# Local deformable attention: one dense read per tile, one write per head, values stored by quarters, loads on ScalarE's queue

## Chip, core and metric

The kernel runs on one core of a Trainium2 chip. The metric is the device time of one execution in microseconds. Before the change three runs took 7693.72, 7705.02 and 7705.33 us; their median, 7705.02 us, is the time to which the change is compared.

The engines by their names in the profile: PE is TensorE (matmuls and transposes; PEld are its weight loads), DVE is VectorE, ACT is ScalarE, POOL is GpSimd, SP is SyncE, which only issues DMAs. ACT issues DMAs too, in order with its own arithmetic (ACTq in the profile).

## What is computed

The program is a network of four blocks, each a "conv" stage and a feed-forward stage with layer norms and residuals, on an input of 4 x 64 x 64 x 128 numbers in float32. Only the first stage, deformable attention, is touched. Cut to what matters:

```python
# q, k, v: layer norm, 1x1 conv, depthwise 3x3 conv; 4 heads g of 32 channels, dilations 1, 3, 5, 7
# per head: 9 taps, each with an offset (y, x) and one mask, made from q by small convs
k_s = deform_sample(k, offset, mask, dilation, pad)   # bilinear: 4 neighbours, 0 outside the image
v_s = deform_sample(v, offset, mask, dilation, pad)
attn = softmax(sum_c(q * k_s) * 32 ** -0.5)           # over the 9 taps
out = sum_taps(attn * v_s);  y = proj(out) + x
```

A sampled value is a weighted sum of pixels. When every offset is at most 1 in size, the pixels that a tap can touch are a 3 x 3 patch around its undisturbed place, with weights that are products of a "hat" in y and a "hat" in x. This is the local part; a branch at run time takes a general path where an offset is larger. With the given inputs the local part runs.

## The kernel before, in words

`stage_deformable` (L366) has two parts.

**Projection** (`deformable_project`, L394 to L606). For each of 4 images: norm (L478, its inputs loaded at L483), q, k, v by matmul and depthwise matmuls (L514), stores to device memory: queries `qd`, keys `kd` (L529), values `vd` (L571, [column, row, channel] with a zero border), offsets and masks `od` (L594). It then reduces the largest offset and loads it into registers (L606), and the branch follows.

**Local part** (`deformable_near`, L609 to L970). A tile T is 128 pixels (two image rows), a chunk c is four tiles; there are 128 tiles and 32 chunks. Its stages:

- `hats` and `hat_products` (L688, L705; POOL): the hats of a chunk from its offsets, times the masks `mk`, and their 3 x 3 products `H`, nine weights per tap.
- `products` (L713; POOL) copies the queries of one tile into a zero-padded weight tile `qm`, of which there are two. `product` (L738; PE, 32 matmuls by 4 heads x 2 halves x 4 blocks, 64 records per tile at L750) multiplies it by bands of keys; `copy_products` (L756; ACT) moves the four results from PSUM to `band`. PSUM has one set of these accumulators, so the next tile's `product` waits for this copy.
- `attention` (L762; DVE): a band covers more columns and rows than a pixel needs; predicated copies shift it by pixel, one copy by row (L768, by bit 3 of the partition's masks) and three by columns (L771, by 4, 2 and 1). Then come the products with `H` (L775), the sum (L782) and the softmax's maximum.
- `spread` (L795): ACT takes the exponential (L798), DVE normalises and writes attn x H into `A`, laid out per pixel as a window of columns with 4 rows (L805 to L818). Partitions of odd image rows are written one row further on by the DMA (`3 * r` in L829).
- `write` (L820; SP): `A` to a scratch memory `dd`, 16 DMAs per chunk (4 heads x 4 groups of 32 partitions), two scratch memories per head in turn.
- `read_dense` (L833): `dd` is read back with each partition's start moved by one pixel, which makes a dense row of weights over a common window of pixels: 4 DMAs per tile, heads 0 and 2 on SP's queue and heads 1 and 3 on ACT's.
- `value_block` (L842; SP): a block of 4 image rows of values, 4 DMAs of 256 KB, one for each quarter q of the columns.
- `transpose` (L862; PE, copies `dt` by ACT), `weigh` (L874; PE, 96 small matmuls), then per chunk the copy of the output (L900), the load of the input `xg` for the residual (L904, SP), its sum with the bias (L905, POOL), `projection` (L908) and, one step later, `store` (L918, SP).

**The order.** The loop of L934 runs steps T = 0 to 141. In a step it emits the stages of different tiles: `products(T+1)`, `hats`, `attention`, `spread`, `write` of chunks at steps 0, 4, 7 and 9 after their first tile, `read_dense` 12 steps and `transpose`/`weigh` 14 steps (`LAG`) after. `behind()` ties the PE blocks to their order and all else behind the last block. The framework's planner turns this into one instruction list per engine from its own cost estimates; each engine then works through its list in order and waits where data or a buffer isn't there. So a DMA that must wait also holds what stands behind it on its engine. Inputs of the local part (`of`, `q`, `kpad`) are loaded at L686, L736 and L729, all by SP.

Of the kernel before, what the change touches and what calls it, by code (L numbers as in the profile page):

```python
# [365 lines left out]
def stage_deformable(k, x, y, w_qkv, b_qkv, w_dw, b_dw, pconv, w_offT, b_off, grid, masks, w_proj, b_proj):  # L366
# [13 lines left out]
    with ExitStack() as octx:  # L380
# [6 lines left out]
        far = deformable_project(k, fp, x, qd, kd, vd, od, w_qkv, b_qkv, w_dw, b_dw, pconv, w_offT, b_off)  # L387
        with tc.If(far > 0) as branch:
            deformable_general(k, x, y, w_qkv, b_qkv, w_dw, b_dw, pconv, w_offT, b_off, grid, w_proj, b_proj)
        with branch.Else():  # L390
            deformable_near(k, dr, x, y, qd, kd, vd, od, masks, w_proj, b_proj)


def deformable_project(k, fp, x, qd, kd, vd, od, w_qkv, b_qkv, w_dw, b_dw, pconv, w_offT, b_off):  # L394
# [9 lines left out]
    with ExitStack() as ctx:  # L404
# [129 lines left out]
        for b in range(4):  # L534
# [57 lines left out]
            for i in range(4):  # L592
                r, h = divmod(i, 2)
                nc.sync.dma_start(od[b][64 * h + 32 * r : 64 * h + 32 * r + 32], off[32 * i : 32 * i + 32])  # L594

# [13 lines left out]
def deformable_near(k, dr, x, y, qd, kd, vd, od, masks, w_proj, b_proj):  # L609
# [23 lines left out]
    PP = [12 * (15 + w) for w in W]  # L633
    with ExitStack() as ctx:
# [14 lines left out]
        for t in qms:  # L649
            nc.gpsimd.memset(t, 0.0)  # L650

# [5 lines left out]

        dd = [[dr.tile([128, 4 * PP[g] + 12], F32, tag=f"dd{i}{g}", name=f"dd{i}{g}") for g in range(4)] for i in range(2)]

        dense = [wp.tile([128, 4, 384], F32, tag=f"D{i}", name=f"D{i}") for i in range(4)]  # L660
        for t in dense:
            nc.gpsimd.memset(t, 0.0)
        for i in range(2):
            for g in range(4):
                zero = dense[g].rearrange("p t n -> p (t n)")
                eng = (nc.sync, nc.scalar)[g % 2]
                eng.dma_start(dd[i][g][:, 0 : 4 * PP[g]], zero[:, 0 : 4 * PP[g]])
                eng.dma_start(dd[i][g][:, 4 * PP[g] : 4 * PP[g] + 12], zero[:, 0:12])

        Hs, bands, outs, vblocks, logits, ofs, hat_of, queries = {}, {}, {}, {}, {}, {}, {}, {}  # L670
        accs, lefts, project, stores = {}, {}, [], []
        last = [None]
# [10 lines left out]
        def offsets(c):  # L683
            b, c8 = divmod(c, 8)
            ofs[c] = sm.tile([128, 4, 81], F32, tag="of", name="of")
            nc.sync.dma_start(ofs[c], od[b][:, 4 * c8 : 4 * c8 + 4, :])  # L686

        def hats(c):  # L688
# [10 lines left out]
            mk = sm.tile([128, 3, 4, 3], F32, tag="mk", name="mk")  # L699
            nc.gpsimd.tensor_copy(mk, window(of, 72, [[3, 3], [81, 4], [1, 3]]))  # L700
            hy = hat[:, 0:4].rearrange("p s a t n i -> p s (a t n) i")
            nc.gpsimd.tensor_tensor(hy, hy, window(mk, 0, [[0, 4], [1, 36], [0, 3]]), op=ALU.mult)
            Hs[c] = sm.tile([128, 4, 36, 9], F32, tag="H", name="H", bufs=3)

        def hat_products(c, groups):  # L705
            H, hat = Hs[c], hat_of[c]
            for g in groups:
                nc.gpsimd.tensor_tensor(
                    H[:, g].rearrange("p n (a c) -> p n a c", a=3), window(hat, 108 * g, [[3, 36], [1, 3], [0, 3]]),
                    window(hat, 108 * (4 + g), [[3, 36], [0, 3], [1, 3]]), op=ALU.mult,  # L710
                )
# [14 lines left out]
        def rows_of_keys(n):  # L726

            b, h = divmod(n, 4)
            nc.sync.dma_start(  # L729
                kpad[:, 8 + 16 * h : 24 + 16 * h, 8:72], kd[b].rearrange("p (y x) -> p y x", x=64)[:, 16 * h : 16 * h + 16, :]  # L730
            )

        def rows_of_queries(n):
            b, h = divmod(n, 8)
            queries[n] = sm.tile([128, 8, 64], F32, tag="q", name="q")
            nc.sync.dma_start(queries[n], qd[b].rearrange("p (y x) -> p y x", x=64)[:, 8 * h : 8 * h + 8, :])  # L736
# [25 lines left out]
        def attention(c):  # L762
            H, band = Hs[c], bands.pop(c)
            prod = sm.tile([128, 4, 36, 9], F32, tag="prod", name="prod", bufs=1)
            for g in range(4):
                rows = lambda off, dims: window(band[g], off, [[4 * CW[g], 12]] + dims)
                n = 3 * CW[g]
                nc.vector.copy_predicated(rows(0, [[1, n]]), bit[:, 0, :, 3:4].to_broadcast([128, 12, n]), rows(CW[g], [[1, n]]))  # L768
                for i, s in enumerate((4, 2, 1)):
                    n = W[g] + s - 1  # L770
                    nc.vector.copy_predicated(  # L771
                        rows(0, [[CW[g], 3], [1, n]]), bit[:, :, :, i : i + 1].to_broadcast([128, 12, 3, n]), rows(s, [[CW[g], 3], [1, n]])
                    )
                for tx in range(3):
                    nc.vector.tensor_tensor(  # L775
                        window(prod, 324 * g + 9 * tx, [[27, 12], [3, 3], [1, 3]]),
                        window(band[g], DIL[g] * tx, [[4 * CW[g], 12], [CW[g], 3], [1, 3]]),
                        window(H, 324 * g + 9 * tx, [[27, 12], [3, 3], [1, 3]]), op=ALU.mult,
# [16 lines left out]
        def spread(c):  # L795
# [7 lines left out]
            for g in range(1, 4):  # L803
                for ty in range(3):
                    nc.vector.tensor_tensor(  # L805
                        window(A[g], ty, [[12 * DIL[g], 12], [3, 3], [12, 3]]), window(H, 324 * g + 108 * ty, [[9, 12], [3, 3], [1, 3]]),
                        window(lg, 36 * g + 12 * ty, [[1, 12], [0, 3], [0, 3]]), op=ALU.mult,
                    )

            t0 = sm.tile([128, 36, 9], F32, tag="t0", name="t0", bufs=1)  # L810
            nc.vector.tensor_tensor(t0, H[:, 0], window(lg, 0, [[1, 36], [0, 9]]), op=ALU.mult)
            for ty in range(3):
                a0 = lambda m0, n: window(A[0], 12 * m0 + ty, [[60, 4], [12, n], [3, 3]])
                tap = lambda tx, s0, n: window(t0, 108 * ty + 9 * tx + s0, [[27, 4], [1, n], [3, 3]])
# [5 lines left out]
        def write(c):  # L820
            A = As[c % 2]
            for g in (1, 2, 3, 0):
                d, P = dd[c % 2][g], PP[g]
                for j in range(4):
                    r = j % 2
                    nc.sync.dma_start(
                        bass.AP(
                            d.tensor, d.offset + 32 * j * (4 * P + 12) + 3 * r, [[4 * P + 12, 32], [P, 4], [1, 12 * W[g]]]
                        ),  # L829
                        A[g][32 * j : 32 * j + 32, :, 0 : W[g]].rearrange("p t c s a -> p t (c s a)"),  # L830
                    )

        def read_dense(T):  # L833
            c, t = divmod(T, 4)
            for g, d in enumerate(DIL):
                m, P = dd[c % 2][g], PP[g]
                (nc.sync, nc.scalar)[g % 2].dma_start(
                    dense[t][:, g, 12 * (7 - d) : 12 * (7 - d) + P],
                    bass.AP(m.tensor, m.offset + t * P, [[16 * (4 * P + 12), 8], [4 * P, 16], [1, P]]),
                )  # L840

        def value_block(n):  # L842
# [4 lines left out]
            d = vd[b]  # L847
            for q in range(4):
                nc.sync.dma_start(
                    t[:, q].rearrange("p s c -> p (s c)"),  # L850
                    bass.AP(d.tensor, d.offset + 16 * q * 10752 + 4 * kb * 128, [[10752, 32], [128, 4], [1, 512]]),
                )
            vblocks[b, kb] = t

        def values(T):
# [3 lines left out]
            if T % 4 == 0:  # L859
                outs[0] = ps.tile([128, 4, 128], F32, tag="out", name="out")  # L860

        def transpose(T):  # L862
            D = dense[T % 4]
            lefts[T] = []
            for ty in range(3):
# [3 lines left out]
                dt = sm.tile([128, 4, 128], F32, tag="dt", name="dt", bufs=4)  # L869
# [4 lines left out]
        def weigh(T):  # L874
# [8 lines left out]
            for q in range(4):  # L883
                for n in range(3):
                    for g in range(4):
                        if n < len(taps[g]):
                            ty, kb, si = taps[g][n]
                            ins = nc.tensor.matmul(
                                quarter(outs[0][32 * g : 32 * g + 32, T % 4, :], q), vblocks[b, kb][:, q, si, 32 * g : 32 * g + 32],
# [5 lines left out]
        def values_done(T):  # L895
            b, i = divmod(T, 32)
            if T % 4 == 3:
# [5 lines left out]
                xg = sm.tile([128, 4, 128], F32, tag="xg", name="xg")  # L903
# [1703 lines left out]
```

## Time and profile before

| What | Value |
|---|---|
| Median of 3 runs | 7705.02 us |
| The profiled execution: its own time, its span | 7690.3 us, 7688.3 us |
| Mean granted clock of PE over the span | 0.892 |
| Projection | 0 to 666 us of the span |
| First `product`, first `transpose`, last `transpose` | 685.2, 778.1 and 1825.0 us |
| The other stages of the network | from about 1830 us on |
| PE, DVE, ACT, POOL busy over the span | 85%, 63%, 35%, 23% |

How to read it: the page cuts the span into 40 slices of 192 us; the local part fills slices 4 to 10. "Busy" of an engine is the time of its instructions, without waits. Beside a line of idle time stands what ended it. Times inside the span come from one profiled execution, so a sum over them is to be set against 7690.3 us, which is 14.7 us under the median of the runs.

### The profile page before, as it was taken

How to read it: one execution, taken by the hardware profiler on the slowest of the kernel's cores; microseconds unless marked ns; L12 is line 12 of the kernel's file. 1: busy time of each engine (PE TensorE's matmuls, PEld its weight loads, DVE VectorE, ACT ScalarE, POOL GpSimd, SP SyncE). 2: the span in 40 equal slices, each digit the busy share in tenths (PEclk: the TensorE clock that was granted, in tenths of full speed). 3: DMA queues.
4: the chain of work that ended last, by engine and by line, in shares of the span. 5: the costliest groups of instructions: out<-in, count | busy, mean ns of one | idle time of the engine just before them, and what ended most of it. 6: DMA issues, size and time to landing. Idle time of an engine off the chain costs nothing. (4 is left out here: it accounts for less than half of the span.)

```text
span 7688.3 us, 157708 instructions
## 1 busy us (share of the span) xinstructions
PE 6522.7 (85%) x63791; PEld 3542.4 (46%) x63791; DVE 4821.5 (63%) x11178; ACT 2690.3 (35%) x6141; POOL 1741.4 (23%) x1634
## 2 busy tenths in 40 slices
PE   7995777775688868989989999798898997997989
PEld 3343666663455644345555555445225234242244
DVE  2113766764277554858856656674785875867877
ACT  3331333333234313611146555565104013031056
POOL 0003444320001100035532221154012112120135
PEclk9997887887799889999999988798897997988989
DMA  4436677775400022030100000001111111111101
GB/s 121 98 87 179 187 209 205 213 199 172 143 4 1 2 60 48 10 117 22 27 12 10 9 10 6 9 1 30 39 25 49 26 33 40 25 35 38 25 23 31
DMA packets 678781, 495.59 MB, mean 64 GB/s; under 512 B 302326, under 2 KB 594104, under 8 KB 674200
## 3 DMA queue, kind: packets, MB, share of 16 engines
q1 hardware_dynamic: 480910, 354.59, 17.0%
q10 hardware_dynamic: 197130, 130.77, 6.2%
q8 instruction: 509, 8.34, 0.5%
q14 instruction: 232, 1.90, 0.1%
HBM read 335.28 MB, written 149.75 MB: 63 GB/s over the span
## 5 line engine op out<-in xcount | busy, mean ns | idle before, releaser
L2476 DVE TENSOR_TENSOR t<-S,q 128x1536 f32<-128x1536 f32 (+3 forms) x608 | 1156.9, 1948 | 123.2 <-PE S L2464 117.9
L2464 PE MATMUL S<-R,L 32*128 32x512 f32 x4096 | 734.6, 651 | 90.3 <-DMA R<-wd 78.9
L2492 PE MATMUL acc<-t,sum 128*32 128x512 f32 x4096 | 639.5, 608 | 0.0
L750 PE MATMUL S<-kpad,qm 32*64 32x240 f32 (+3 forms) x8192 | 403.4, 421 | 216.0 <-ACT band L760 97.5
L2178 PE MATMUL pe<-ew,yT 128*128 128x512 f32 x1024 | 479.4, 603 | 27.4 <-DVE xs L2184 24.5
L1777 PE MATMUL acc<-w,attT 128*64 128x264 f32 x4096 | 486.3, 391 | 10.4 <-DVE w L1773 10.4
L2464 PEld LDWEIGHTS S<-R,L 32*128 32x128 f32 x4096 | 200.6, 186 | 611.4 <-issue 280.4
L2498 ACT COPY agg<-acc 128x512 f32<-128x512 f32 x32 | 18.8, 586 | 1194.0 <-DMA L<-pd 626.7
L750 PEld LDWEIGHTS S<-kpad,qm 32*64 32x64 f32 x8192 | 299.9, 156 | 271.5 <-issue 136.9
L1770 POOL TENSOR_TENSOR w<-xtl,ei 128x528 f32<-128x528 f32 x256 | 332.1, 1319 | 309.6 <-ACT ei L1769 204.5
L2184 DVE SCALAR_TENSOR_TENSOR xs<-pe,gate,xs 128x128 f32<-128x128 f32 x1024 | 332.5, 345 | 96.5 <-PE pe L2178 79.8
L1773 DVE TENSOR_TENSOR w<-xtl,pe 128x1056 f32<-128x1056 f32 x256 | 320.3, 1251 | 100.3 <-ACT ei L1769 89.4
L1777 PEld LDWEIGHTS acc<-w,attT 128*64 128x64 f32 x4096 | 284.0, 137 | 197.5 <-DVE w L1774 38.0
L2187 ACT ACTIVATE sc<-pe,gate 128x128 f32<-128x128 f32 x1024 | 291.3, 374 | 202.2 <-PE pe L2178 194.1
L514 PE MATMUL dw<-pad,diag 32*32 32x512 f32 x6912 | 310.4, 614 | 12.9 <-issue 7.0
L2507 POOL TENSOR_TENSOR o<-o,bf 128x512 f32<-128x512 f32 x32 | 40.7, 1271 | 1229.4 <-ACT o L2506 1229.4
L760 ACT COPY band<-S 128x144 f32<-128x144 f32 (+3 forms) x512 | 136.0, 351 | 480.4 <-DMA D<-dd 152.3
L2492 PEld LDWEIGHTS acc<-t,sum 128*32 128x32 f32 x4096 | 92.7, 108 | 458.4 <-issue 436.1
L2178 PEld LDWEIGHTS pe<-ew,yT 128*128 128x128 f32 x1024 | 185.6, 193 | 234.3 <-issue 151.4
L768 DVE COPY_PREDICATED band<-bit,band 128x432 f32<-128x432 int32 (+3 forms) x128 | 107.5, 895 | 270.0 <-ACT band L760 264.2
L868 PE MATMUL pt<-ident,D 128*128 128x128 f32 x1536 | 243.0, 315 | 29.2 <-DMA D<-dd 15.2
L771 DVE COPY_PREDICATED band<-bit,band 128x288 f32<-128x288 int32 (+11 forms) x384 | 243.0, 742 | 0.0
(520 smaller groups left out, 13065.8 us busy)
## 6 DMA issues: line engine op xcount, KB each, us to landing
vb<-vd SPq DMA_DIRECT2D x272, 256.0 KB
D<-dd ACTq DMA_DIRECT2D x128, 192.0 KB
D<-dd SPq DMA_DIRECT2D x128, 168.0 KB
D<-dd ACTq DMA_DIRECT2D x128, 144.0 KB
w<-in_e_weight_dram ACTq DMA_DIRECT2D x16, 1024.0 KB
w<-in_e_weight_dram SPq DMA_DIRECT2D x16, 1024.0 KB
wd<-s SPq DMA_DIRECT2D x32, 512.0 KB
D<-dd SPq DMA_DIRECT2D x128, 120.0 KB
```

What stands on the lines that cost most here:

```text
L514: nc.tensor.matmul(acc[g][32 * c : 32 * c + 32], diag[r, j, tap, :], pads[j][r, y0 : y0 + 8, tx : tx + 64], start=(tap == 0), stop=(tap == 8),
L750: ins = nc.tensor.matmul(acc[g][64 * h : 64 * h + 64].rearrange("p (a s) c -> p a s c", a=3), qm[rows, h, m, :], keys, start=(m == 0), sto ...
L771: nc.vector.copy_predicated(rows(0, [[CW[g], 3], [1, n]]), bit[:, :, :, i : i + 1].to_broadcast([128, 12, 3, n]), rows(s, [[CW[g], 3], [1, ...
L1770: nc.gpsimd.tensor_tensor(w2[:, 2:4], xt[:, 2:4, 0:2], window(ei, 0, [[0, 2], [0, 2], [1, 132]]), op=ALU.mult)
L1773: nc.vector.tensor_tensor(w1, xt[:, :, 1:3], window(pe, 0, [[0, 4], [0, 2], [1, 132]]), op=ALU.mult)
L1777: nc.tensor.matmul(acc[b // 2][64 * (b % 2) : 64 * (b % 2) + 64], attT[:, b // 2, hp, 64 * (b % 2) : 64 * (b % 2) + 64], src[:, b].rearran ...
L2178: nc.tensor.matmul(pe[h].rearrange("p e c -> p (e c)"), yT[:, 128 * t : 128 * t + 128], ew[:, 4 * h : 4 * h + 4, :].rearrange("p e c -> p ...
L2184: nc.vector.scalar_tensor_tensor(xt, pe[0][:, e, :], gate[:, t, e : e + 1], xt, op0=ALU.mult, op1=ALU.add)
L2187: nc.scalar.activation(sc[:, e, j, :], pe[1][:, e, :], AF.Copy, scale=gate[:, t, 4 + e : 5 + e])
L2464: nc.tensor.matmul(S[:, j, :], Ls[n % 2][r, ag, :], Rs[n % 2][r, ag].rearrange("p x y -> p (x y)"), start=True, stop=True)
L2476: nc.vector.tensor_tensor(t[:, j0:j1].rearrange("p u (x y) -> p u x y", x=8), S[:, j0:j1].rearrange("p u (x y) -> p u x y", x=8), qf[:, q0 ...
L2492: nc.tensor.matmul(acc[0][32 * h : 32 * h + 32, :], sum4, t[:, j, :], start=(u < 4), stop=(u >= 60))
```

## The change

The scratch memory gets one layout for all heads: per pixel-row of 128 partitions, 4 tiles x 4 heads x 384 numbers. Four DMAs write it per chunk (one per head, all 128 partitions), one DMA per tile reads it, and there are three such memories in turn. Since a write no longer moves odd rows by one, `H` gets four rows of weights: the first three or the last three are filled, by the masks times (1 - row) and times row; the row shift (L768) goes, the column shifts work on all 48 rows of a band. Values are copied a second time in the projection, device memory to device memory, by quarters (`vq`), and a block of values is then one DMA. Loads of offsets, keys, queries and of `xg` are issued by ACT; `xg` is loaded at the start of a chunk's first `weigh` step, not after its last; offsets are loaded a step earlier; stores are issued two steps after the projection or later. `H` has 2 buffers (before 3), `dt` 3 (before 4).

```diff
+        vq = [dr.tile([32, 84, 4, 128], F32, tag=f"vq{b}", name=f"vq{b}") for b in range(4)]
...
                 nc.sync.dma_start(od[b][64 * h + 32 * r : 64 * h + 32 * r + 32], off[32 * i : 32 * i + 32])
+            for q in range(4):
+                nc.sync.dma_start(vq[b][:, :, q, :], vd[b][16 * q : 16 * q + 32])
...
-    PP = [12 * (15 + w) for w in W]
+    ROW = 4 * 4 * 384 + 12
...
-        dd = [[dr.tile([128, 4 * PP[g] + 12], F32, tag=f"dd{i}{g}", name=f"dd{i}{g}") for g in range(4)] for i in range(2)]
+        dd = [dr.tile([128, ROW], F32, tag=f"dd{i}", name=f"dd{i}") for i in range(3)]
...
-        for t in dense:
-            nc.gpsimd.memset(t, 0.0)
-        for i in range(2):
-            for g in range(4):
...
+        nc.gpsimd.memset(dense[0], 0.0)
+        zero = dense[0].rearrange("p g n -> p (g n)")
+        for d in dd:
+            for t in range(4):
+                nc.scalar.dma_start(d[:, 1536 * t : 1536 * t + 1536], zero)
+            nc.scalar.dma_start(d[:, 6144:ROW], zero[:, 0:12])
...
-            nc.gpsimd.tensor_copy(mk, window(of, 72, [[3, 3], [81, 4], [1, 3]]))
+            nc.gpsimd.tensor_copy(mk[:, 0].rearrange("p (a t n) -> p a t n", a=3, t=4), window(of, 72, [[3, 3], [81, 4], [1, 3]]))
+            nc.gpsimd.tensor_scalar(mk[:, 1], mk[:, 0], row, None, op0=ALU.mult)
+            nc.gpsimd.tensor_tensor(mk[:, 0], mk[:, 0], mk[:, 1], op=ALU.subtract)
             hy = hat[:, 0:4].rearrange("p s a t n i -> p s (a t n) i")
-            nc.gpsimd.tensor_tensor(hy, hy, window(mk, 0, [[0, 4], [1, 36], [0, 3]]), op=ALU.mult)
-            Hs[c] = sm.tile([128, 4, 36, 9], F32, tag="H", name="H", bufs=3)
+            h4 = hy_of[c] = sm.tile([128, 4, 36, 4], F32, tag="hy", name="hy", bufs=1)
+            nc.gpsimd.tensor_tensor(h4[:, :, :, 0:3], hy, at(0), op=ALU.mult)
+            nc.gpsimd.tensor_tensor(hy, hy, at(1), op=ALU.mult)
+            nc.gpsimd.tensor_tensor(h4[:, :, :, 1:3], h4[:, :, :, 1:3], hy[:, :, :, 0:2], op=ALU.add)
+            nc.gpsimd.tensor_copy(h4[:, :, :, 3], hy[:, :, :, 2])
+            Hs[c] = sm.tile([128, 4, 36, 12], F32, tag="H", name="H")
...
-                nc.vector.copy_predicated(rows(0, [[1, n]]), bit[:, 0, :, 3:4].to_broadcast([128, 12, n]), rows(CW[g], [[1, n]]))
                 for i, s in enumerate((4, 2, 1)):
                     n = W[g] + s - 1
-                    nc.vector.copy_predicated(
-                        rows(0, [[CW[g], 3], [1, n]]), bit[:, :, :, i : i + 1].to_broadcast([128, 12, 3, n]), rows(s, [[CW[g], 3], [1, n]])
-                    )
+                    nc.vector.copy_predicated(flat[:, :, 0:n], bit[:, 0, :, i : i + 1].to_broadcast([128, 48, n]), flat[:, :, s : s + n])
...
         def write(c):
-            for g in (1, 2, 3, 0):
-                for j in range(4):
...
+            for g, d in enumerate(DIL):
+                m = dd[c % 3]
+                nc.sync.dma_start(
+                    bass.AP(m.tensor, m.offset + 384 * g + 12 * (7 - d), [[ROW, 128], [1536, 4], [1, 12 * W[g]]]),
+                    As[c % 2][g][:, :, 0 : W[g]].rearrange("p t c s a -> p t (c s a)"),
+                )
...
         def read_dense(T):
-            for g, d in enumerate(DIL):
-                (nc.sync, nc.scalar)[g % 2].dma_start(
...
+            m = dd[c % 3]
+            nc.sync.dma_start(
+                dense[t].rearrange("p g n -> p (g n)"), bass.AP(m.tensor, m.offset + 1536 * t, [[16 * ROW, 8], [ROW - 12, 16], [1, 1536]])
+            )
...
         def value_block(n):
-            for q in range(4):
-                nc.sync.dma_start(
...
+            d = vq[b]
+            nc.sync.dma_start(
+                t.rearrange("p s q c -> p (s q c)"), bass.AP(d.tensor, d.offset + 4 * kb * 512, [[84 * 512, 32], [512, 4], [1, 2048]])
+            )
...
         def values(T):
...
             if T % 4 == 0:
                 outs[0] = ps.tile([128, 4, 128], F32, tag="out", name="out")
+                inputs[0] = sm.tile([128, 4, 128], F32, tag="xg", name="xg")
+                nc.scalar.dma_start(inputs[0], tokens(x, b, i, 4))
...
-                step(T, -2, offsets, 4)
+                step(T, -3, offsets, 4)
...
-            late = list(stores)
+            late = [o for o in stores if o[0] <= T - 2]
```

`rows_of_keys`, `rows_of_queries` and `offsets` change from `nc.sync` to `nc.scalar` and nothing else. In `hat_products`, `attention` and `spread` the nine weights per tap become twelve (`[3, 3]` becomes `[3, 4]` or `[4, 3]` in the access patterns), with the same number of instructions beside the removed L768.

## The prediction

> **What bounds the kernel now.** I read the slices first, to see what sort of stretch the local part is. In these rows PE's busy share, its granted clock, and the DMA engines' share stand in tenths; the local part is slices 4 to 10.
>
> ```profile
> PE   7995777775688868989989999798898997997989
> PEclk9997887887799889999999988798897997988989
> DMA  4436677775400022030100000001111111111101
> ```
>
> PE is busy for 7 tenths, at a clock of about 8, while the DMA engines are busy for 7 tenths too: nothing is full. The second view gives the busy time of PE, PEld, DVE, ACT and POOL in four stretches, then clock, DMA share and GB/s:
>
> ```profile
> 224.00:273.00 49.00, 47.52 (x353) 14.78 (x354) 11.55 (x75) 32.61 (x64) 0.00 (x0) 0.93 0.22 61
> 690.00:780.00 90.00, 48.76 (x863) 36.87 (x871) 65.76 (x139) 17.62 (x61) 65.87 (x82) 0.70 0.69 203
> 780.00:1750.00 970.00, 733.11 (x19481) 612.47 (x19464) 645.76 (x1629) 327.05 (x878) 379.88 (x541) 0.83 0.72 204
> 1750.00:1830.00 80.00, 53.38 (x1594) 46.96 (x1592) 19.53 (x57) 28.25 (x55) 8.10 (x7) 0.85 0.56 168
> ```
>
> The steady stretch, 780 to 1750 us, holds tiles 14 to 127 of the product: 114 steps or 28.5 chunks, so 970 / 28.5 = 34.0 us a chunk. Per chunk PE is busy 25.7, DVE 22.7, POOL 13.3, ACT 11.5 us, the DMA engines 0.72 x 34.0 = 24.5 us. So the period is made by waits. The list of waits in that stretch names them (who waited, for whom: total, times, longest):
>
> ```profile
> POOL xg L905 <- DMA xg<-in_x_dram: 351.3, 20, 23.4
> ACT band L760 <- DMA D<-dd: 145.6, 28, 8.3
> PE S L750 <- ACT band L760: 89.0, 41, 5.7
> ACT lg L798 <- DMA D<-dd: 82.6, 11, 9.4
> PE S L750 <- POOL qm L721: 60.6, 16, 8.4
> ACT lg L798 <- DMA kpad<-kd: 49.0, 6, 10.6
> ```
>
> L798 is an exponential; it reads neither keys nor dense rows. It stands behind a DMA issue on ACT that had to wait. The timeline of one chunk shows the whole knot:
>
> ```profile
> 1203.52 2.57 PE L750 MATMUL S<-kpad,qm 32*64 32x144 f32 x64
> ...
> 1218.27 0.46 SPq L904 DMA_DIRECT2D xg<-in_x_dram  x1
> ...
> 1220.04 1.44 ACTq L837 DMA_DIRECT2D D<-dd  x2
> 1221.52 0.32 ACT L798 ACTIVATE lg<-lg 128x144 f32<-128x144 f32 x1 [9.65 <-DMA xg<-in_x_dram]
> 1221.75 1.04 ACT L760 COPY band<-S 128x144 f32<-128x144 f32 x4
> 1222.16 4.82 PE L750 MATMUL S<-kpad,qm 32*64 32x144 f32 x64 [5.15 <-ACT band L760]
> 1223.68 1.34 POOL L905 TENSOR_TENSOR xg<-xg,bpj 128x512 f32<-128x512 f32 x1 [16.64 <-DMA xg<-in_x_dram]
> ```
>
> SP reaches the load of `xg` late, behind writes and value loads. ACT's two reads wait (by the trace's inference until that load has landed), ACT stands for 9.65 us, the accumulators aren't copied, PE waits 5.15 us, and the product after the gap takes 4.82 instead of 2.57 us. POOL meanwhile stands 16.64 us.
>
> **The change, part by part**, per chunk in the steady stretch.
>
> *DMA issues.* By the medians of the lines' own rows (write L826 431 ns, read L837 598, values L849 602, about 450 for the small loads), SP spends 16 x 0.43 + 8 x 0.60 + 8.1 x 0.60 + 3.5 x 0.45 + 0.38 (store) = 18.5 us on issuing; after, 4 x 0.43 + 4 x 0.60 + 2.0 x 0.60 + 0.38 = 5.7. ACT's 8 reads (8 x 0.58 = 4.7 us, and the waits above: 145.6 + 82.6 + 49.0 = 277 us, 9.7 a chunk) become 3.5 small loads, 1.6 us. What those wait for is old: keys for a product that the copy ahead of them on ACT waits for anyway, queries and offsets for a buffer of two chunks ago, `xg` for a store issued two steps earlier. If they do wait, the exponential, the copies to `band` and `dt` stand behind them, and PE behind these.
>
> *The load of `xg`* moves from the end of the chunk's four weighing steps to their start, on the other queue. 351 us of POOL's waiting goes, and with it most of PE's 60.6 us for `qm`. What is late next on POOL is its own work.
>
> [...] The row: the steady stretch moves 204 GB/s at a share of 0.72 through both queues together. [...] I credit the order of the load, not its queue; no term below counts bandwidth for it.
>
> *PE.* At full clock a step takes 5.0 us (transposes 1201.96 to the next ones at 1206.99, without a gap), a chunk 4 x 5.0 + 2.1 (projection, L911) = 22 us. No instruction is added.
>
> *DVE.* L768 goes: 36.4 + 31.0 + 26.0 + 21.1 = 114.5 us over 32 chunks, 3.6 a chunk. The twelve shifts grow by a third: their sizes sum to 5328 elements, so 1776 more; from 612 elements (980 ns) to 180 (527 ns) one costs 1.05 ns: +1.9. Products L775 (12 x 36 more), reduction L782 (432 more), L805 (9 x 36), L811 (108), L815 to L818 (108) have 1404 more elements, at about 1.04 ns +1.5. Sum -0.2: nothing.
>
> *POOL.* Two operations of 36 (mask copy L700: 0.33 each), a second product by the mask (L702: 1.0), one addition of 288 (L697: 0.76), a copy of 144 (between L700's 0.33 and L698's 0.63: 0.4), four products of 432 in place of 324 (1.0 against 0.815: +0.76): +3.6 us, 13.3 to 17. Within a period of 25 that hides. Where it doesn't: small copies L816 take 0.17 us alone and 0.77 beside POOL's products (median 239, longest 1290 ns), so at worst all 3.6 us fall on DVE: 22.7 to 26.3.
>
> *DMA bytes.* A dense tile grows from 192 + 168 + 144 + 120 = 624 KB to 768 KB, a chunk from 34.0 us x 204 GB/s = 6.94 to 7.53 MB. At the present 204 / 0.72 = 283 GB/s per full share this is 26.6 us; if the 5.3 MB of dense rows and values, in rows of 6 and 8 KB, run as fast as 680 to 690 us do (377 GB/s at 1.07, that is 352) and the rest as in the projection (107 at 0.46, that is 233), 15.1 + 9.6 = 24.7.
>
> *Period after.* PE 22, DVE 22.5 to 26.3, DMA 24.7 to 26.6: three within a fifth of each other never overlap wholly, and nothing above 26.6 is left as a wait of its own, so I take 27, bounds 25 and 32. Steady: 28.5 x (27 - 34) = **-200 us** (-257 to -57).
>
> *The last 14 steps* (80 us, `transpose` and `weigh` alone): one read and an earlier `xg`: -5, bounds -15 and 0.
>
> *The copies to `vq`* (16 of 1344 KB in pieces of 512 B). No row copies memory to memory. The nearest: the eight loads L554 (8 x 500 KB, pieces of 252 B) hold SP 21 us, 190 KB a us, so 5376 KB an image take 28 us; below, at 352 GB/s, 16; above, if each byte costs for reading and for writing, 56. For images 0 to 2 SP has room: after the stores L594 end at 224.5 us it has only two loads (249.7) before 273.5, and the DMA share there is 0.22. So +3 us, bounds 0 and 75 (at 56 the norm's loads come 25 us late for each). For image 3 they stand on SP ahead of the register load and the local part's first lines.
>
> *The start.* Zeros grow from 5.1 to 9.5 MB, 4.4 MB at 377 GB/s = 12 us, all on ACT, whose first copy already waits 34.8 us for them; the last `vq` copies share the engines. Against it, 16 + 16 issues per chunk shrink in a stretch of 90 us where SP spends 11.2 us on one chunk's writes and 10 on reads. I take +10, bounds -15 and +35. `dt` and `H` with a buffer less: a `dt` is free once the weighing ahead has run, `H` of two chunks ago once its spread has; POOL already waits 35 us for that in all: 0, up to +30.
>
> Sum: -200 - 5 + 3 + 10 = -192, so 7690.3 becomes 7498. The runs' median lies 14.7 us above that execution, their lowest 3.4; with about 12 of it I forecast **7510 us**.
>
> **Rivals.**
> 1. *Some of the knot stays* (0.20): another load takes the waiting place, ACT's `xg` behind its store or a read behind its four writes, which now all must land before one DMA. For it: SP stays in order, and 123 us of its waits in the stretch are writes behind dense reads. The period ends at 30 to 32: -114 to -57, so about 7595 to 7650.
> 2. *Deeper* (0.08): DVE's bound of 22.5 holds and DMA runs at its best, 24.7 a chunk: -265 and a start 15 us shorter, 7400 to 7430.
> 3. *Slower* (0.12): the `vq` copies lie open. Place: SP and the shared engines at the end of each image. Price: 4 x 56 = 224 us, against the -192: about +32, 7735. It decides from some 48 us of open time an image. Against it: the 49 us of room at 224 to 273.
> 4. *No change* (0.06): an unseen wait of PE keeps the period; "issue" ends 60 us of its idle time before L888, which the change doesn't name. 7690 to 7720.
>
> **The numbers.** The forecast (period 25 to 29) has 0.54. Faster by over 0.2% (15 us, about what a measurement of this kernel can tell): 0.54 + 0.20 + 0.08 = 0.82; within: 0.06; slower: 0.12. The range 7420 to 7650 takes the forecast, rival 1 and half of rival 2.
>
> **What the profile after should show.** `xg L905 <- DMA xg` gone from POOL's waits; no DMA ahead of L760 and L798; SP's issues for a chunk under 8 us; PE's clock in the steady stretch about 0.9, products near 2.6 us; DMA share 0.85 or more; DVE's busy time there within 5% of 646 us. Last `transpose` at about 1635 us. I am wrong if the first product starts after 720 us, if DVE's busy time grows by a tenth, or if the period is above 30 with ACT or SP still held by a DMA.

## The result and the profile after

The changed kernel takes 8020.93 us (median of 4 runs, 8003.6 to 8058.26) beside 7699.37 us (4 runs) of the kernel before: ratio 1.0425, 95% interval 1.0384 to 1.0467. The forecast was 7510. The profiled execution took 8032.4 us (span 8030.6), 342 us more than the one before.

Where the 342 us lie can be read from one pair of rows. The view of tile `xg` gives the first and the last start of POOL's sum `xg<-xg,o`, which closes each of the 32 chunks (columns: least, median and longest duration in ns, then first and last start). Before, then after:

```profile
L914 POOL TENSOR_TENSOR xg<-xg,o x32: 1262/1272/1289, 820.4 to 1829.6; 128x512 f32<-128x512 f32 x32
```

```profile
L915 POOL TENSOR_TENSOR xg<-xg,o x32: 1259/1266/1341, 888.7 to 2152.7; 128x512 f32<-128x512 f32 x32
```

The first chunk closes 68 us later. The 31 periods that follow grow from 1009.2 / 31 = 32.6 us to 1264.0 / 31 = 40.8 us, 255 us in all. What comes after is 19 us longer, in stages that the change doesn't touch (over all kernels of this document this part lies between 5845.6 and 5885.3 us, so 19 us say nothing). I use this "period" for every kernel below; by it the 34.0 of the prediction is 32.6.

The stretches 690 to 780 and 780 to 1750 us of the kernel after, with the columns of the prediction:

```profile
690.00:780.00 90.00, 32.36 (x493) 25.46 (x498) 20.20 (x44) 9.08 (x30) 40.30 (x57) 0.56 0.65 231
780.00:1750.00 970.00, 595.98 (x14696) 493.50 (x14681) 535.75 (x1204) 260.29 (x674) 367.59 (x562) 0.73 0.68 170
```

Everything is less busy: PE 596 us in place of 733, the DMA engines' share 0.68 in place of 0.72, and the granted clock, forecast at 0.9, fell to 0.73. The waits of the same stretch (who waited, for whom: total, times, longest):

```profile
DVE band L782 <- ACT band L773: 416.9, 23, 26.9
POOL xg L906 <- DMA xg<-in_x_dram: 402.9, 19, 24.1
ACT band L773 <- PE S L763: 248.1, 63, 10.4
...
PE S L763 <- POOL qm L734: 151.6, 22, 16.1
```

The first row that I said would go, POOL's wait for `xg`, is longer than before (402.9 in place of 351.3 us). The timeline of one chunk shows its shape:

```profile
1421.58 1.28 POOL L915 TENSOR_TENSOR xg<-xg,o 128x512 f32<-128x512 f32 x1
1422.89 0.36 SPq L922 DMA_DIRECT2D x<-xg  x1
...
1425.23 0.39 ACTq L862 DMA_DIRECT2D xg<-in_x_dram  x1
1425.66 1.07 ACT L773 COPY band<-S 128x144 f32<-128x144 f32 x4 [8.74 <-PE pt L870]
...
1444.25 1.26 POOL L906 TENSOR_TENSOR xg<-xg,bpj 128x512 f32<-128x512 f32 x1 [21.39 <-DMA xg<-in_x_dram]
...
1445.83 2.67 PE L763 MATMUL S<-kpad,qm 32*64 32x144 f32 x47 [6.08 <-POOL qm L734]
```

This is a ring through three in-order engines. POOL closes a chunk, SP stores it, ACT can load the next `xg` into that buffer only when the store has landed (2.3 us later), the load lands 19 us after its issue, and POOL's bias sum waits 21.39 us for it with the copies of queries behind it, so PE waits too. The second finding is in the windows view of a stretch in which, by the packets' records, 98% of the bytes are 6144-byte pieces of two dense reads:

```profile
1312.50:1315.00 2.50, 0.00 (x0) 0.00 (x0) 2.40 (x9) 0.00 (x0) 0.51 (x1) 0.50 0.52 206
```

The DMA share (second number from the right) is 0.52 and the rate 206 GB/s: reads are queued, yet half of the 16 engines' time is unused. The packets' records have 8 to 10 packets in flight at any moment of this stretch, 8.2 as a mean. These two readings are theory B (ring) and theory A (half the engines). The 8 engines of theory A are an estimate from this stretch, 0.52 x 16 = 8.3 engines' time and 8.2 packets; that it is the same 8 in every read, no run shows.

### The profile page after: what moved, and what is told of

Read it like the earlier page. It is cut to its first block, busy times and chain, and to the rows that moved or that the text cites. A ratio compares the mean times of both kernels' runs of the same rounds, so it can differ in the third digit from the quotient of the medians.

```text
span 8030.6 us, 156368 instructions
## 1 busy us (share of the span) xinstructions
PE 6582.9 (82%) x63791; PEld 3591.8 (45%) x63791; DVE 4834.0 (60%) x11051; ACT 2704.6 (34%) x6141; POOL 1800.7 (22%) x1791
## 5 line engine op out<-in xcount | busy, mean ns | idle before, releaser
L763 PE MATMUL S<-kpad,qm 32*64 32x288 f32 (+3 forms) x8192 | 433.3, 458 | 425.8 <-POOL qm L734 227.2
L782 DVE COPY_PREDICATED band<-bit,band 128x384 f32<-128x384 int32 (+11 forms) x384 | 316.0, 936 | 639.4 <-ACT band L773 570.5
L763 PEld LDWEIGHTS S<-kpad,qm 32*64 32x64 f32 x8192 | 324.4, 172 | 488.5 <-POOL qm L734 245.7
L1779 PEld LDWEIGHTS acc<-w,attT 128*64 128x64 f32 x4096 | 283.5, 137 | 198.8 <-DVE w L1776 38.7
L870 PE MATMUL pt<-ident,D 128*128 128x128 f32 x1536 | 272.0, 342 | 33.4 <-issue 21.0
L872 ACT COPY dt<-pt 128x512 f32<-128x512 f32 x384 | 210.0, 603 | 242.4 <-PE pt L870 225.2
```

Source lines behind the costliest of these rows:

```text
L763: ins = nc.tensor.matmul(acc[g][64 * h : 64 * h + 64].rearrange("p (a s) c -> p a s c", a=3), qm[rows, h, m, :], keys, start=(m == 0), sto ...
L782: nc.vector.copy_predicated(flat[:, :, 0:n], bit[:, 0, :, i : i + 1].to_broadcast([128, 48, n]), flat[:, :, s : s + n])
L1779: nc.tensor.matmul(acc[b // 2][64 * (b % 2) : 64 * (b % 2) + 64], attT[:, b // 2, hp, 64 * (b % 2) : 64 * (b % 2) + 64], src[:, b].rearran ...
```

## The experiments

The kernel before was timed again beside each group of kernels; its medians there lie between 7693.7 and 7709.6 us. All 18 kernels, together with the two of the change ("First `xg+o`" is the start of the first `xg<-xg,o`; both columns on the right come from the profiled execution):

| Kernel | Median us | Ratio to before, 95% interval | First `xg+o` | Period |
|---|---|---|---|---|
| before | 7699.4 | | 820 | 32.6 |
| after | 8020.9 | 1.0384 to 1.0467 | 889 | 40.8 |
| wide | 7919.9 | 1.0265 to 1.0299 | 882 | 37.4 |
| wide_k8 | 8161.2 | 1.0569 to 1.0652 | 927 | 43.8 |
| nobias | 8016.5 | 1.0381 to 1.0416 | 897 | 40.2 |
| loads_sp | 8006.4 | 1.0370 to 1.0404 | 889 | 40.5 |
| split | 7968.6 | 1.0332 to 1.0384 | 895 | 38.8 |
| dense_only | 7986.4 | 1.0343 to 1.0378 | 880 | 40.5 |
| dense_only_split | 7846.9 | 1.0159 to 1.0228 | 876 | 35.8 |
| dense_only_624 | 7842.4 | 1.0169 to 1.0223 | 882 | 35.6 |
| wide_xgold | 7730.5 | 1.0016 to 1.0047 | 888 | 31.4 |
| wide_xg3 | 7936.1 | 1.0288 to 1.0322 | 883 | 37.8 |
| wide_xg3_nobias | 7918.2 | 1.0266 to 1.0301 | 887 | 37.3 |
| wide_xgold_nobias | 7825.1 | 1.0137 to 1.0175 | 884 | 34.4 |
| wide_xgold_h3 | 7734.8 | 1.0037 to 1.0070 | 891 | 31.3 |
| wide_xgold_h3_nobias | 7834.6 | 1.0157 to 1.0208 | 891 | 34.1 |
| wide_xgold_qmact | 7715.4 | 1.0023 to 1.0054 | 889 | 31.0 |
| before_xgact | 7727.8 | 1.0016 to 1.0043 | 820 | 33.4 |
| before_vq | 7703.5 | 0.9998 to 1.0022 | 836 | 32.1 |
| before_wide | 7889.4 | 1.0215 to 1.0262 | 822 | 38.7 |

**wide: the skew in the writes, plain rows in the read.**

```diff
-                    bass.AP(m.tensor, m.offset + 384 * g + 12 * (7 - d), [[ROW, 128], [1536, 4], [1, 12 * W[g]]]),
+                for t in range(4):
...
+                        bass.AP(m.tensor, m.offset + 1536 * t + 384 * g + 12 * (7 - d), [[16 * ROW, 8], [ROW + 12, 16], [1, 12 * W[g]]]),
...
-                dense[t].rearrange("p g n -> p (g n)"), bass.AP(m.tensor, m.offset + 1536 * t, [[16 * ROW, 8], [ROW - 12, 16], [1, 1536]])
+                dense[t].rearrange("p g n -> p (g n)"), bass.AP(m.tensor, m.offset + 1536 * t, [[ROW, 128], [1, 1536]])
```

> The changed kernel with one edit: the skew of a pixel per partition is made by the writes (16 per chunk, one per head and tile, outermost dimension 8), so that the dense read is 128 plain rows. Nothing is left out. Theory A (the read's address pattern has 8 as its outermost dimension, so the 768 KB of a dense tile travel on 8 of the 16 DMA engines, and those 8 set the period): a read's 128 packets are spread over 16 engines, about 400 GB/s while only dense rows move in place of 197; the period falls from 43 to 36 us or less, 28.5 x 7 = 200 us, so 7820 us or less. Theory B (a ring through three in-order queues sets the period: POOL's bias sum L906 waits for the load of xg, that for ACT, that for SP's store, that for POOL): the ring is untouched, POOL's wait at the bias sum stays above 450 us of the steady stretch, and the time stays within 60 us of 8020.

Measured 7919.9, 101 us less than the changed kernel; the period fell by 3.4 us, not by 7. Both theories missed the size. The 8 is now the outermost dimension of the writes, which carry 264 KB a tile in place of the read's 768. A part of the loss is in the read's pattern, and something else now holds the period: ACT's wait for the store ahead of the copies to `band` grew from 70.7 to 205.0 us in 900 to 1750 us:

```profile
ACT band L772 <- DMA x<-xg: 205.0, 21, 10.7
```

**wide_k8: the same bytes and pieces, 8 as the outermost dimension again.** The memory gets 64 bytes between parts of 16 rows, so that the read takes parts and rows as two dimensions.

```diff
+    EIGHTH = 16 * ROW + 16
...
-                dense[t].rearrange("p g n -> p (g n)"), bass.AP(m.tensor, m.offset + 1536 * t, [[ROW, 128], [1, 1536]])
+                dense[t].rearrange("p g n -> p (g n)"), bass.AP(m.tensor, m.offset + 1536 * t, [[EIGHTH, 8], [ROW, 16], [1, 1536]])
```

> The kernel 'wide' with one edit: each scratch memory is laid out as 8 parts of 16 rows with 64 bytes between the parts, so that the dense read's outermost dimension is 8 again. Same bytes, same pieces of 6144 bytes, same 16 writes. Nothing is left out. Theory A (a read with 8 as its outermost dimension uses 8 of the 16 DMA engines, and these bound the changed kernel): the dense read is slow again, the time goes back from 7920 to 7980 to 8040 us. Rival (the gain of 'wide' came from its smaller writes or from the plain rows): 7900 to 7940 us.

Measured 8161.2: 241 us above `wide`, more than expected. 45 us of it are the start, where the zeros were written in the same pattern (ACT's first copy to `band` came at 773.7 us, in `wide` at 736.0); the period rose from 37.4 to 43.8 us, 31 x 6.4 = 200 us. The rival is out. The windows view of stretches with hardly anything but dense pieces, first wide_k8, then wide:

```profile
1092.00:1095.50 3.50, 3.50 (x85) 2.55 (x77) 3.01 (x11) 0.87 (x4) 0.00 (x0) 0.50 0.52 145
```

```profile
1177.50:1179.50 2.00, 1.96 (x56) 1.52 (x55) 2.00 (x3) 0.00 (x0) 0.00 (x0) 1.00 1.02 419
```

Half the share with the 8, the whole with 128 rows. The packets' records show why: 8 to 10 packets are in flight at any moment in the first stretch, 16 to 18 in the second. A 6144-byte packet took 238 ns in `wide` and 244 ns in the 206 GB/s stretch of the changed kernel, so there half as many packets run, each as fast. That it took 352 ns in the stretch of `wide_k8`, hence 145 GB/s, isn't explained. The two rows and the 8 and 16 packets agree with theory A's 8 of 16 engines; which 8 they are, no run here shows.

**nobias: the bias by PE, POOL's L906 gone.**

```diff
-                nc.gpsimd.tensor_tensor(xg, xg, bpj.to_broadcast([128, 4, 128]), op=ALU.add)
+                nc.tensor.matmul(pr[:, j, :], k.ones_row, bpj[0:1, 0, :], start=True, stop=False)
```

> The changed kernel with one edit: the bias is added by PE in the projection (a matmul of one row of ones ahead of each of the four), and POOL's sum of xg and bias (L906) goes, so that POOL first touches xg at the end of a chunk. Nothing is left out. Theory A (dense read on 8 DMA engines): those engines carry the same bytes, the period stays at 41 to 43 us, 7960 to 8020 us. Theory B (ring through L906): POOL's wait of 538 us in the steady stretch goes with no wait as long in its place, the products' wait for qm (208 us) falls under 60, the period falls to 34 or less: 7770 us or less.

**loads_sp: the four small loads issued by SP**, the same edit for `of`, `kpad`, `q` and `xg`:

```diff
-            nc.scalar.dma_start(ofs[c], od[b][:, 4 * c8 : 4 * c8 + 4, :])
+            nc.sync.dma_start(ofs[c], od[b][:, 4 * c8 : 4 * c8 + 4, :])
```

> The changed kernel with one edit: offsets, keys, queries and xg (still at the start of a chunk) are issued by SP in place of ACT. Nothing is left out. Theory A: the same bytes on the same 8 engines, 7980 to 8040 us. Theory B: the ring keeps POOL and SP but loses ACT's part (some 7 us of the 19 from a store's issue to the landing of xg), if the loads don't stand behind dense reads instead: 7820 to 7960 us. A third theory (loads of small pieces suffer on a queue of their own beside 6 KB pieces): the loads land sooner after their issue than the 17 us of the changed kernel.

Measured 8016.5 and 8006.4, period 40.2 and 40.5. With the read's pattern in place, neither taking POOL out of the ring nor taking ACT out gains anything, as theory A says. `nobias` isn't a clean test, though: PE's wait for `qm` (141.7 us in 900 to 1750) went, as theory B said, but ACT's wait for the store grew from 70.7 to 153.4 us, and PE now waits at the projection's first matmul, that of the bias:

```profile
PE pr L911 <- ACT dt L872: 61.1, 20, 5.2
```

**dense_only: all undone but the dense part.** Beside the lines that go back to the kernel before for values, loads and `xg`:

```diff
-                nc.sync.dma_start(vq[b][:, :, q, :], vd[b][16 * q : 16 * q + 32])
...
-            late = [o for o in stores if o[0] <= T - 2]
+            late = list(stores)
```

> The changed kernel with all undone but the dense part: values come by four DMAs from vd again (no vq), offsets, keys, queries and xg are loaded by SP, xg at the end of a chunk, stores without the delay. What stays: one scratch layout with four writes and one read a tile, three memories, twelve weights a tap. Nothing is left out. Theory A: the 8 engines carry 768 KB a tile in place of 624, so the period is 23% above the 34 of before, up to 41: 7850 to 7920 us. Theory B: without the early load of xg there is no ring, SP issues fewer DMAs, and the time is that of before or less: 7550 to 7720 us.

Measured 7986.4, period 40.5. The dense part without any of the other edits holds 277 of the 321 us. It is above even theory A's range.

**wide_xgold: wide, and `xg` loaded by SP at the end of the chunk again.**

```diff
-                inputs[0] = sm.tile([128, 4, 128], F32, tag="xg", name="xg")
-                nc.scalar.dma_start(inputs[0], tokens(x, b, i, 4))
...
-                xg = inputs[0]
+                xg = sm.tile([128, 4, 128], F32, tag="xg", name="xg")
+                nc.sync.dma_start(xg, tokens(x, b, 4 * c, 4))
```

> The kernel 'wide' with the move of xg undone: SP loads it at the end of a chunk's weighing, as before the change. Nothing is left out. Theory B as the second bound (once the engines are evenly used, the wait of ACT for the load of xg, which waits for SP's store, 10 us a chunk ahead of the copies to band, sets the period of 37 us): ACT's 205 us of waiting for the store goes, the period falls by 5 to 9 us, 7660 to 7780 us. Rival (the bytes or PE's lower clock keep the period): 7860 us or more.

Measured 7730.5, as theory B says for the second bound: the period falls from 37.4 to 31.4 us, below the kernel before. So the two findings are two limits of one period, about 41 and 37 us, and undoing the lower alone shows nothing. The two edits together take back 101 + 189 = 290 of the 321 us.

**wide_xg3 and wide_xg3_nobias: a third buffer for `xg`**, then the bias by PE as well.

```diff
-                inputs[0] = sm.tile([128, 4, 128], F32, tag="xg", name="xg")
+                inputs[0] = sm.tile([128, 4, 128], F32, tag="xg", name="xg", bufs=3)
```

> The kernel 'wide' with three buffers for xg in place of two (room comes from t0, which takes the memory of prod). Nothing is left out. Theory B: the load of a chunk's xg no longer waits for the store of the chunk just ended but for one 34 us older; ACT's wait for the store (205 us in 850) and POOL's at the bias sum (244) go, the period falls to 30 or less, 7600 to 7720 us. Rival (bytes or clock): 7860 us or more.

> The kernel 'wide_xg3' with the bias added by PE in the projection, so that POOL's L906 goes too. Nothing is left out. Theory B: POOL has nothing left that waits for xg ahead of the copies of queries; if the ring was broken by the third buffer this is worth the 1.3 us of L906 a chunk at most, so within 40 us of 'wide_xg3', faster. If POOL's bias sum still waited there, it is worth up to 100 us more.

Measured 7936.1 and 7918.2, no gain: theory B's detail was wrong. The timeline of wide_xg3 shows why:

```profile
1294.49 0.38 SPq L922 DMA_DIRECT2D x<-xg  x1
...
1297.01 0.39 ACTq L862 DMA_DIRECT2D xg<-in_x_dram  x1
1297.44 0.28 ACT L772 COPY band<-S 128x144 f32<-128x144 f32 x1 [10.06 <-DMA x<-xg]
```

The load again stands right behind a store, 2.5 us. ACT's load for a chunk had moved up by one chunk: behind the store of chunk 11 comes the load of chunk 14, in `wide` that of chunk 13. So, it seems, the planner places it as early as a buffer comes free by its own estimate, and so where it has to wait.

**before_xgact and before_vq: one part of the change alone in the kernel before**, word for word from its diff: the two lines of `values` that make and load `xg`; the copies to `vq` with `value_block` and the index order in `weigh`.

> The kernel before with one part of the change alone: xg is loaded by ACT, named at the start of a chunk's weighing. Nothing is left out. Theory B (the planner puts that load on ACT right behind the store that frees the buffer, so ACT stands for the store's landing, and POOL's bias sum ahead of the copies of queries): slower, a period of 36 to 38, 7760 to 7820 us. The prediction's theory (an early load takes POOL's wait of 351 us away): faster, 7600 to 7680 us.

> The kernel before with one part of the change alone: vd is copied to vq by quarters in the projection, and a block of values is one DMA of 8 KB rows in place of four of 2 KB. Nothing is left out. Prediction and present theory agree on a small size: the copies lie in the projection's slack and cost 4 us for images 0 to 2 and up to 15 for the last, the single DMA saves SP 3.6 us of issues a chunk that are not the bound: 7690 to 7740 us. [...]

Measured 7727.8 (ratio 1.0016 to 1.0043) and 7703.5 (0.9998 to 1.0022). The early load costs by itself, but 0.8 us a period and not the 4 that I expected; 137 us of ACT's wait for the store appear in 900 to 1750 us, and POOL's wait for `xg` falls from 310 to 177. The values by quarters cost nothing in all that can be measured: first `xg+o` 16 us later, the period 0.5 us shorter.

**before_wide: the kernel before with plain rows**, at 32 writes a chunk in place of 16.

```diff
-                            d.tensor, d.offset + 32 * j * (4 * P + 12) + 3 * r, [[4 * P + 12, 32], [P, 4], [1, 12 * W[g]]]
+                            d.tensor, d.offset + 16 * j * (4 * P + 12) + 3 * r, [[4 * P + 24, 16], [P, 4], [1, 12 * W[g]]]
...
-                    bass.AP(m.tensor, m.offset + t * P, [[16 * (4 * P + 12), 8], [4 * P, 16], [1, P]]),
+                    bass.AP(m.tensor, m.offset + t * P, [[4 * P + 12, 128], [1, P]]),
```

> The kernel before with one edit: the skew of a pixel per partition is made by the writes (32 per chunk, of 16 partitions each, in place of 16), and the dense reads are 128 plain rows. Nothing is left out. Theory A (the kernel before was itself bound by 8 DMA engines: by the packets' times the dense rows take 349 of 700 us on 8 engines, the rest 336, together 98%): the period falls from 34 to 32 or less though SP issues 7 us a chunk more, 7580 to 7650 us. Rival (the period before came from the waits for xg on POOL and ACT): 7690 to 7730 us, or slower by SP's issues, up to 7800.

Measured 7889.4, slower, and it doesn't decide: the timeline of SP shows a new bound.

```profile
1319.76 0.94 SPq L837 DMA_DIRECT2D D<-dd  x2
1320.79 23.50 SPq L826 DMA_DIRECT2D dd<-A  x32
1344.39 0.84 SPq L837 DMA_DIRECT2D D<-dd  x2
```

The 32 writes hold SP for 23.5 us, and nothing is left between its issues. Whether the kernel before was bound by 8 engines stays open.

**dense_only_split and dense_only_624: the dense read on two queues**, in two DMAs of 768 numbers; then in four DMAs of the heads' own widths, as `read_dense` had them before. The first:

```diff
-            nc.sync.dma_start(
-                dense[t].rearrange("p g n -> p (g n)"), bass.AP(m.tensor, m.offset + 1536 * t, [[16 * ROW, 8], [ROW - 12, 16], [1, 1536]])
-            )
+            for h in range(2):
+                (nc.sync, nc.scalar)[h].dma_start(
+                    dense[t][:, 2 * h : 2 * h + 2].rearrange("p g n -> p (g n)"),
+                    bass.AP(m.tensor, m.offset + 1536 * t + 768 * h, [[16 * ROW, 8], [ROW - 12, 16], [1, 768]]),
+                )
```

> The kernel 'dense_only' with each dense read in two DMAs of two heads, one on SP and one on ACT (same bytes, pieces of 3072 bytes, still 8 as the outermost dimension). Nothing is left out. Theory A1 (bytes on 8 engines): no change, 7940 to 8020 us. Theory A2 (a 768 KB read on one queue lets values and loads of that queue wait behind it on 8 engines): the second queue lets them pass, 7780 to 7900 us.

> The kernel 'dense_only' with the dense read in four DMAs of the heads' own widths, alternating on SP and ACT as before the change (624 KB a tile; all four dense tiles are set to zero at the start). Nothing is left out. Theories A1 and A2 together: the time goes back to 7700 to 7780 us. If it stays above 7850, the cost of 'dense_only' lies neither in bytes nor in queues but in the rest (four writes that all must land, three memories, twelve weights with two buffers of H).

Measured 7846.9 and 7842.4. The split gains 140 us, in theory A2's range: bytes on 8 engines alone (A1) don't hold `dense_only`, since the same bytes, still with 8 as the outermost dimension, run at a period of 35.8 in place of 40.5. The fewer bytes of `dense_only_624`, in smaller pieces and twice as many reads, gain nothing beyond. About half of the cost of `dense_only` thus goes with the single 768 KB read on one queue; the split also halves the pieces, and this is not separated. The time of the issues themselves isn't small either: in 900 to 1750 us SP's issues take 474 us in `dense_only` (a write up to 9.3 us), 25.6 a chunk, and 306 in `dense_only_split`, 13.9 a chunk, though SP issues as many DMAs a chunk in both. Why an issue takes that long, no run shows. `dense_only_624` lies between the two ranges that were expected. The rest, 148 us, was not taken apart: 62 of it is the start (first `xg+o` 882 for 820).

**split: the same two queues in the changed kernel.**

> The changed kernel with one edit: each dense read is two DMAs of two heads, one on SP and one on ACT (same bytes, pieces of 3072 bytes, 8 as the outermost dimension). Nothing is left out. If the single queue bounds the changed kernel, the period falls until ACT's load of xg behind the store holds it (the 37 us of 'wide'): 7890 to 7960 us. If bytes on 8 engines alone bound it: 7990 us or more.

Measured 7968.6, 52 us gained (the intervals of the two ratios just touch), period 38.8. ACT's wait for the store is then 219.3 us in 900 to 1750, as in `wide`, so that it holds the period is likely but not tested. It landed between the two expectations' ranges.

**wide_xgold_nobias, wide_xgold_h3, wide_xgold_h3_nobias, wide_xgold_qmact: what holds `wide_xgold`.** The bias by PE as in nobias; a third buffer of `H` with six value blocks; both; the copies to `qm` by ACT.

```diff
-            Hs[c] = sm.tile([128, 4, 36, 12], F32, tag="H", name="H")
+            Hs[c] = sm.tile([128, 4, 36, 12], F32, tag="H", name="H", bufs=3)
...
-                nc.gpsimd.tensor_copy(
+                nc.scalar.copy(
                     window(qm, 256 * h, [[32, 2], [72, 4], [1, 8]]),
```

> The kernel 'wide_xgold' with the bias added by PE in the projection, so that POOL no longer has a sum that waits for xg (217 us of 850 in 'wide_xgold') ahead of the copies of queries (for which PE waits 133 us there). Nothing is left out. If that wait is what now sets the period of 31 us: 28 to 29 us, 7620 to 7690 us. Rival (the wait passes to the second use of xg or to another): 7710 us or more.

> The kernel 'wide_xgold' with three buffers of H, as before the change, in place of two (room comes from a value block less, six in place of seven). Nothing is left out. If POOL's wait for H (88 us of 850) delays the copies of queries for which PE waits 133 us: 7640 to 7700 us. If the bias sum's wait for xg (217 us) is what delays them: within 25 us of 7730.

> The kernel 'wide_xgold_nobias' with three buffers of H and six of values. Nothing is left out. In 'wide_xgold_nobias' POOL waited 194 us of 850 for H's second buffer with the copies of queries behind it. If that is why it lost 95 us to 'wide_xgold', the third buffer gives it back and more: 7600 to 7690 us, faster than both kernels. If not: 7780 us or more.

> The kernel 'wide_xgold' with the copies of queries into qm made by ACT in place of POOL. Nothing is left out. If POOL's order (bias sum and products of hats ahead of these copies) holds PE's products (133 us of PE's waits in 850): the period falls from 31 to 28 to 30, 7620 to 7700 us, faster than or equal to the kernel before. Rival (ACT's own 0.5 us a tile and its order, behind dt and loads, cost as much): 7710 to 7800 us.

Measured 7825.1, 7734.8, 7834.6 and 7715.4. Removing POOL's bias sum made it slower twice. It did remove what it was meant to: PE's wait for `qm`, 132.7 us in 900 to 1750, went. But PE waits at the bias matmul for ACT's copies `dt`, 98.1 us in place of 26.9 at the projection before:

```profile
PE pr L910 <- ACT dt L870: 98.1, 23, 5.8
```

POOL's wait for `H`'s buffer also grew, from 88 to 194 us. The third buffer of `H` changed nothing: that wait stayed at 91 without the edit of the bias and at 222 with it. Which of the two waits costs the 95 us stays open. The copies by ACT gave 0.3 us a period. None beats the kernel before: where the bias stays on POOL, 31.0 to 31.4 us a chunk are 37 to 47 us less over 31 periods, but the start costs 68 to 70.

## Why the prediction was wrong

**The step that failed first is "DMA bytes".** It took the DMA engines' share as room on 16 equal engines and got a floor of 24.7 to 26.6 us. The dense read's pattern, 8 x 16 rows, used half of the engines' time where it ran alone (0.52, 8.2 packets in flight). From the packets of 1000 to 1700 us I estimate: dense pieces 187.7 us as a mean over 16 engines, so 375 on 8 of them; all others 295.8; together 671 of 700 us, 96%, at a share of 0.69 (if the dense pieces keep to the same 8 engines, which no run shows, and the others are spread evenly). By this estimate the 8 engines had hardly any room in this stretch. The same estimate for the kernel before gives 98%, which I didn't make, since the share of 0.72 looked like room. It is no floor for the period, though: a packet's time isn't fixed (a 6144-byte piece took 374 ns as a mean here, 276 in `wide`), and `dense_only_split` ran at 35.8 us with the same dense bytes, still with 8 as the outermost dimension. `wide` and `wide_k8` show that the pattern costs this much (-101 and +241 us); how the cost divides between the 8 engines' time and what waits behind a slow read on its queue stays open.

**"The load of `xg`" failed second.** It credited POOL's 351 us and called what ACT's loads wait for "old ... a store issued two steps earlier". The order in which the loop emits the steps says that; the planned order doesn't: the load stands 2.3 us behind the store that frees its buffer, on an engine with the copies to `band` behind it. `wide` to `wide_xgold` prices it at 189 us once the read has plain rows (share 0.59 in place of 0.69 in 900 to 1750 us); in the kernel before it was 28. Rival 1 named the place, "ACT's `xg` load behind its store", but priced it as a smaller gain. By `before_xgact` it is a loss by itself.

**The start** was +10 (at most +35) and was +68. The trace of ACT shows the zeros of three memories, all on its queue, and the loads of keys behind them:

```profile
690.85 15.67 ACTq L672 DMA_DIRECT2D dd<-D  x4
...
728.57 11.56 ACTq L742 DMA_DIRECT2D kpad<-kd  x3
740.25 0.28 ACT L773 COPY band<-S 128x144 f32<-128x144 f32 x1 [76.33 <-issue]
```

Before, the copies to `band` began here:

```profile
694.96 1.07 ACT L760 COPY band<-S 128x144 f32<-128x144 f32 x4 [34.77 <-DMA dd<-D]
```

The first copy comes at 740.3 in place of 695.0 us. The bytes were counted, the queue behind them wasn't: a load of offsets follows, and POOL waits 20.36 us for it before it copies the next queries. This is read from the trace; no kernel tried fewer zeros, but `wide_k8`, which wrote the same zeros in the slow pattern, started 45 us later than `wide`. 16 us of the start go with the `vq` copies (`before_vq`), which stand ahead of the branch.

**"Slower"** was given 0.12 for the `vq` copies, the wrong mechanism: `before_vq` costs nothing measurable in all, 16 us at the start against 0.5 us less a period (the projection's last stores of `od` came 3.7 us later in the changed kernel, forecast +3).

**What held:** SP's issues fell as counted (by their durations in 900 to 1750 from 21.9 us a chunk, where the medians of the prediction gave 18.5, to 5.8, forecast 5.7), but weren't the bound; DVE's busy time over the local part went from 732.8 to 747.8 us, 2% (forecast: nothing), though in `wide_xgold`, at a period of 31.4, the same instructions took 802.4; POOL's grew by 65 us, 2 a chunk (forecast 3.6). Of my three signs of error one came true: the period above 30 with ACT held by a DMA (83.5 us behind the store in 780 to 1750). The first product (705.8 us) did start before 720, and DVE's busy time didn't grow by a tenth.

## What to carry to other kernels

Before a DMA's bytes are set against the DMA engines' share, look at the outermost dimension of its pattern: with an 8 there this read ran at half the share (0.52, with 128 at 1.02), and the mean share of 0.7 hid it. Where two limits lie close together, undo them together as well; the lower alone may show nothing. An early load is early only if the buffer was freed long ago in the engine's final order (here the load stood 2.3 us behind the store), and another buffer doesn't help when the planner moves the load up with it (7936.1 us with three buffers, 7919.9 with two).

## What the runs showed of the hardware

The dense read of 768 KB moved at 206 GB/s and a share of 0.52 with 8 as its outermost dimension, at 419 GB/s and 1.02 with 128. 8 to 10 packets were in flight at a time with the 8, 16 to 18 with the 128, and a packet of 6144 bytes took 244 and 238 ns (in `wide_k8`, again with the 8 and a share of 0.52, 352 ns and 145 GB/s). Its issue on SP took at least 574 ns with the 8 and 315 ns with the 128. The granted clock of three kernels in 780 to 1750 us was 0.73 at a period of 40.8 us (`after`), 0.78 at 37.4 (`wide`) and 0.83 at 32.6 (`before`).
